# A two-layer graph network on one core: the boundary between the layers reworked (residual joins, a separate normalised tile, order of the dots, scores made ahead of their maxima)

## The chip, the cores and the metric

The kernel runs on one core of one Trainium2 chip. The metric is the device time of that core in microseconds (us), the median of several executions. Before the change it is 3235.16 us, the median of three runs between 3231.14 and 3235.99. All arithmetic on tensors is in fp32; masks are kept in bf16.

## The reference

There are 2708 rows of width 1024 and an adjacency matrix `adj`. Cut to what matters:

```python
h = relu(layernorm(x))                        # layer 0
e = relu((h @ Wf + bf) @ (h @ Wg + bg).T)
a = softmax(where(adj > 0, e, NEG), axis=1)
x = x + a @ (h @ W0 + bW)

h = relu(layernorm(x))                        # layer 1
hW = h @ W1
f1, f2 = hW @ a1, hW @ a2
e = leaky_relu(f1 + f2.T, 0.2)
a = softmax(where(adj > 0, e, NEG), axis=1)
x = x + relu(a @ hW)
```

A leaky relu is monotonic. So the largest score of a row of layer 1 is the leaky relu of `f1` plus the largest `f2` among its neighbours. The kernel needs the maximum of `f2` over the neighbours only, not the scores, to find the shift of the softmax. It must know `f2` of all rows before that maximum is final, and the last rows of `x` come out of the last projection of layer 0.

## The kernel before

**Tiles.** The rows are 22 tiles of up to 128 (`NT`), taken in 11 pairs (`NQ`, `pairs`; one pair consists of the two short tiles of 74 rows). The same rows as targets are five panels, 586, 586, 512, 512 and 512 columns wide (`panels`, `width`). Scores lie transposed: source rows on the partitions, targets of one panel along the free axis. Every large product is made by a Strassen scheme with seven products M1 to M7, in the order M1, M5, M2, M6, M3, M7, M4 in `accumulate` (L466), so the two tiles of a pair are its halves.

**Stages.** In layer 0 each panel p goes through `scores` (L917 matmuls), a softmax, `aggregate(0, p)` (L478, TensorE banks `gx`, `gy`, `gz`, `gv`) and `project(0, p)` (L821, banks `px`, `py`, `pz`). The projection multiplies with `W`, and its `finish0` adds the residual `x_res`, stores the new rows `x1_d` (L1083) and calls `rows_done` (L1023). For the rows of the first four panels, `rows_done` puts the moments, the normalisation, two dots and the Strassen sums of the pair (`pair_h`, L253) into a list of deferred work. The two dots give `f[0]` (f1) and `f[1]` (f2) of the row, from the normalised row and the vectors `wab`, which are `W1 @ a1` and `W1 @ a2`. The list is called `later`: `put` appends to it, `behind(rate)` emits what the credit allows between TensorE products, and `flush` empties it.

**The last projection.** It is `project(0, 4, by_pair=True)`. It takes the two pairs of panel 4 one after the other, so that the rows of the first pair are done while the second is multiplied. `rows_done` then doesn't defer: it emits `normalize`, the dots for `f[0]`, the dots for `f[1]`, `raise_max` for panel 0 (L876, `mx` = the larger of `mx` and mask plus f2) and `pair_h` at once. After the last tile `shifts1` (L1005) turns `mx` on TensorE (`column_max`, L646, bank `mx_ps`), reduces it to one maximum per column (`mcol`), and makes two small columns `z` and `m` from f1 and that maximum. `weights1` (L1128) spreads them over the partitions (`spread`, L205: transposes of a broadcast column into `sp_ps`, then a copy on alternately VectorE and ScalarE) into `ub` and `vb`. Then, one tile at a time, it makes the weights `P`: an Identity pass on ScalarE (L1144), a fused add and maximum and the addition of the mask on VectorE, an exp on ScalarE (L1147). The running sum `sm` follows two tiles later. `aggregate(1, 0)` starts with `gx` on the first tile of `P`.

**What sets the order.** A scheduler decides the order on each engine, from the program's order and the dependences, save where an instruction is held in program order (loads, and VectorE within `scores`). Each engine then works through its queue in that order. VectorE's adds and small operations are recorded under one helper, so all of VectorE's instructions show line L44, and one tells them apart by the tile names. SyncE's queue issues all loads (L121), in order. GpSimd's queue issues the stores and adds `bW` to `x_res` (L1078).

**Buffers.** There are 54 equal `slot` buffers (scores, weights, residuals, temporaries), 12 `stream` buffers (operands loaded from HBM), and 8 PSUM banks. A tile's buffer is free when its last reader is done.

**Lines touched.** `normalize` (L242) works in place: its two Relu passes on ScalarE write into the residual tile that `go` in `finish0` has just sent off to `x1_d`. In `project` (L787) the first product is copied from `px` to `pt` by ScalarE (L827), since M2 accumulates into the same bank after that. M5 and M6 are added to this copy; each of M3, M7 and M4 is added to one of the three sums and then to the residual, two additions each:

```python
o = {M3: M6, M7: M5, M4: M1}[m]
add(t(o), ps, t(o))
finish(tb if m != M3 else ta, 0 if m == M4 else 1, t(o))
```

Of the kernel before, what the change touches and what calls it, by code (L numbers as in the profile page):

```python
# [17 lines left out]
ALPHA = 0.2  # L18
# [38 lines left out]
def kernel(  # L57
# [141 lines left out]
    def halves(t):  # L199
        return [t[:, e * W:(e + 1) * W] for e in range(2)]  # L200
# [23 lines left out]
    def columns_of(p, col):  # L224
        return [col[:n, i:i + 1] for i, (_, n) in enumerate(panels[p])]
# [13 lines left out]
        nc.scalar.activation(rs[:n, :1], mv[:n, 1:2], AF.Sqrt, bias=eps[:n])  # L239
        of_rows[id(t)] = mv, rs  # L240

    def normalize(t):  # L242

        n = t[0].shape[0]
        if id(t) not in of_rows:
            moments(t)
        mv, rs = of_rows.pop(id(t))
        nc.vector.reciprocal(rs[:n, :1], rs[:n, :1])
        nc.vector.tensor_scalar(rs[:n, 1:], mv[:n, :1], rs[:n, :1], -1.0, op0=OP.mult, op1=OP.mult)
        for e in range(2):  # L250
            nc.scalar.activation(t[e], t[e], AF.Relu, bias=rs[:n, 1:], scale=rs[:n, :1])

    def pair_h(l, q, ha, hb):  # L253

# [532 lines left out]
    def project(l, p, G, finish, then={}, by_pair=False, rate=2.0):  # L787

        full = width[p] // P
        col = lambda i, n: [t[:, :, i * P:i * P + n] for t in G]  # L790
        todo = [(first[p] + i, first[p] + i + 1, P, col(i, P), col(i + 1, P)) for i in range(0, full, 2)]
        if p == panel_of[short[0]]:
            n = tiles[short[0]][1]
            for e in range(2):
                nc.scalar.copy(carry[:, e, :, :n], G[e][:, :, full * P:full * P + n])
        if p == panel_of[short[1]]:
            n = tiles[short[1]][1]
            todo.append((*short, n, [carry[:, e, :, :n] for e in range(2)], col(full, n)))
        start_of, finish = finish
        ws = {m: load_W(l, m) for m in (M1, M2)}  # L800
        start_of([t for g in todo for t in g[:2]])
        lefts = []
        for ta, tb, n, (a11, a12), (a21, a22) in todo:
            s = [slot(f"ps{i}", (P, NH, P))[:, :, :n] for i in range(4)]
            add(s[0], a21, a22)
            sub(s[1], s[0], a11)
            sub(s[2], a11, a21)
            sub(s[3], a12, s[1])
            lefts.append({M1: a11, M2: a12, M5: s[0], M6: s[1], M7: s[2], M3: s[3], M4: a22})
        for group, left in (zip([[t] for t in todo], [[t] for t in lefts]) if by_pair else [(todo, lefts)]):  # L810
            acc, tmp = {}, {}
            for m in (M1, M2, M5, M6, M3, M7, M4):
                start = m in (M1, M5, M6)
                w_ = ws.pop(m) if m in ws else load_W(l, m)
                which = "x" if m in (M1, M2) else "y" if m in (M5, M3) else "z"
                for i, (ta, tb, n, _, _) in enumerate(group):
                    if start:
                        acc[which, i] = bank(f"p{which}")
                    ps = acc[which, i][:n]
                    for k in range(NH):  # L820
                        nc.tensor.matmul(ps, left[i][m][:, k, :], w_[k], start=(start and k == 0), stop=(k == NH - 1),  # L821
                                         skip_group_check=True)
                    if start:
                        tmp[m, i] = slot(f"pt{m}")
                    t = lambda m: tmp[m, i][:n, :W]
                    if m == M1:
                        nc.scalar.copy(t(M1), ps)  # L827
                    elif m == M2:
                        finish(ta, 0, ps)
                    elif m in (M5, M6):  # L830
                        add(t(m), ps, t(M1))
                    else:
                        o = {M3: M6, M7: M5, M4: M1}[m]
                        add(t(o), ps, t(o))
                        finish(tb if m != M3 else ta, 0 if m == M4 else 1, t(o))
                    behind(rate)
                if m in then:
                    then.pop(m)()
# [166 lines left out]
    def shifts1(p, between=None):  # L1005

        k, t0 = len(panels[p]), first[p]
        top = column_max(p, mx[p], between)[:, :k]
        f1 = f[0][:, t0:t0 + k]
        z, m, c = (stats.tile([P, 5], FP, name=nm)[:, :k] for nm in ("z", "m1", "none"))  # L1010
        nc.vector.tensor_add(z, f1, top)
        nc.vector.scalar_tensor_tensor(m, z, ALPHA, z, op0=OP.mult, op1=OP.max)
        nc.vector.tensor_scalar(c, top, -BIG / 2, None, op0=OP.is_ge)
        nc.vector.tensor_mul(m, m, c)
        nc.vector.tensor_scalar(c, top, -BIG / 2, -BIG, op0=OP.is_lt, op1=OP.mult)
        nc.vector.tensor_add(m, m, c)
        sub(z, f1, m)
        nc.vector.scalar_tensor_tensor(m, f1, ALPHA, m, op0=OP.mult, op1=OP.subtract)
        return z, m

    done_rows, first_mask = {}, {}

    def rows_done(t, xt):  # L1023

        n = tiles[t][1]
        done_rows[t] = xt

        def dots(k):
            dot(f[k][:n, t:t + 1], xt, [b[:n] for b in halves(wab[k])])
            if k == 1:  # L1030
                nc.vector.tensor_scalar(f2s[:n, t:t + 1], f[1][:n, t:t + 1], ALPHA, None, op0=OP.mult)

        q, k = pair_of[t]
        whole = all(s in done_rows for s in pairs[q])
        if panel_of[t] == NP - 1:
            normalize(xt)
            dots(0)
            dots(1)
            raise_max(0, q, k, first_mask[t][:n, :width[0]])
            if whole and q == NQ - 1:  # L1040
                nc.scalar.activation(stats.tile([P, 1], FP, name="warm"), eps, AF.Exp)
            if whole:
                if q == NQ - 1:
                    got["zm"] = shifts1(0, lambda: pair_h(1, q, *(done_rows[s] for s in pairs[q])))
                else:
                    pair_h(1, q, *(done_rows[s] for s in pairs[q]))
                for p in range(1, NP):
                    put_max(p, q)
            return

        def met():
            known.add(q)
            for p in range(NP):
                if generated[p] > q:
                    put_max(p, q)
        put(1.5, lambda: moments(xt))
        put(0.5, lambda: normalize(xt))
        put(1.6, lambda: dots(0))
        put(1.6, lambda: dots(1))
        if whole:  # L1060
            put(2.7, lambda: pair_h(1, q, *(done_rows[s] for s in pairs[q])))
            put(0.0, met)

    def finish0(p):
# [15 lines left out]
        def go(t, e, c):  # L1080
# [3 lines left out]
            seen[t] = seen.get(t, 0) + 1  # L1084
            if seen[t] == 2:
                rows_done(t, xs[t])
        return start, go

    got = {}
    generated = [0] * NP  # L1090

    def take_max(p):
        got["m"] = column_max(p, got["acc"])
# [6 lines left out]
    for p in range(NP):  # L1100
# [4 lines left out]
        if p + 1 < NP:  # L1105
            B = project_q(p + 1, hooks)
        else:
            project(0, p - 1, G.pop(p - 1), finish0(p - 1), hooks)
        if p == 0:
            prepare_W()  # L1110
        then = {}
# [13 lines left out]
    project(0, NP - 1, G.pop(NP - 1), finish0(NP - 1), by_pair=True, rate=0.0)  # L1125


    def weights1(p, z, m):  # L1128

        w = width[p]  # L1130
        ub, vb1, sm = slot("ub"), slot("vb1"), slot("sm")
        spread(ub, columns_of(p, z))
        spread(vb1, columns_of(p, m))
        S = [None] * NT
        order = [(q, k) for k in range(2) for q in range(NQ)]
        exps[0] = 0

        def go(i, mk):
            if i < len(order):
                q, k = order[i]  # L1140
                n, t = rows_of[q], pairs[q][k]
                S[t] = slot("P")
                s = S[t][:n, :w]
                nc.scalar.activation(s, vb1[:n, :w], AF.Identity, bias=f2s[:n, t:t + 1])  # L1144
                nc.vector.scalar_tensor_tensor(s, ub[:n, :w], f[1][:n, t:t + 1], s, op0=OP.add, op1=OP.max)
                add(s, s, mk[0][:n, :w])
                nc.scalar.activation(s, s, AF.Exp)  # L1147
            if i >= LAG:
                q, k = order[i - LAG]
                total(p, sm, S[pairs[q][k]], rows_of[q], i == LAG)  # L1150
            exps[0] += 1

        front = []
        for i in range(len(order) + LAG):
            mk = []
            front.append([2.1, (lambda i=i, mk=mk: mk.append(load_mask(p, *order[i]))) if i < len(order) else None,
                          (lambda i=i, mk=mk: go(i, mk)), False, None])
        later[:0] = front
        return S, sm

    def finish1(p):
# [9 lines left out]
        def go(t, e, c):  # L1171
# [2 lines left out]
            nc.scalar.activation(o, c, AF.Relu)  # L1174
            add(xs[t][e], xs[t][e], o)
            nc.gpsimd.dma_start(out[r0:r0 + n, e * W:(e + 1) * W], xs[t][e])
        return start, go

    def take_shifts(p):
        flush()  # L1180
# [42 lines left out]
```

## Time and profile before

The profiled execution has a span of 3235.3 us with a mean granted clock of 0.987. Some parts of it, in us from its start:

| stretch | from | to | length |
|---|---|---|---|
| aggregate(0, 4) | 2016.5 | 2151 | 134.3 |
| last projection, pair 1 | 2150.8 | 2175.9 | 25.1 |
| last projection, pair 2 | 2175.9 | 2208.5 | 32.6 |
| last product to the first matmul of layer 1's aggregate | 2208.5 | 2233.85 | 25.3 |
| `gx` of aggregate(1, 0), 88 matmuls | 2233.85 | 2257.6 | 23.8 |

A timeline row gives the start, the length, the engine, line and operation, the tiles written and read with their shapes, and how many instructions were taken together; in brackets stand the engine's idle time before it and who released it. A row of waits gives the engine, line and tile, the releaser, the total wait, how many there were, and the longest. A row of windows gives the stretch and then the busy time of each engine with its count of instructions, the clock granted to TensorE (1.00 is full), the share of time that the DMA engines were busy, and GB/s.

### The profile page before, as it was taken

What the parts mean: (1) busy time and instruction counts of PE and PEld (TensorE: products, weight loads), DVE (VectorE), ACT (ScalarE), POOL (GpSimd) and SP (SyncE); (2) the same over time, 40 slices, a digit from 0 to 9 for tenths busy, and PEclk for the clock granted to TensorE, in tenths of its full rate; (3) what the DMA queues carried; (4) which work ended last, traced back from release to release, by engine and by line L of the source; (5) the groups of instructions that cost most, each with busy time, mean ns of one, the idle gap of its engine ahead of it and who ended that gap; (6) DMA issues with size and microseconds to landing.
All of it is one profiled execution on the core that took longest, in us unless ns stands there. A gap on an engine that the chain in (4) does not pass through costs nothing. (4 is left out here: it accounts for less than half of the span.)

```text
span 3235.3 us, 35363 instructions
## 1 busy us (share of the span) xinstructions
PE 3137.1 (97%) x12924; PEld 2333.4 (72%) x12924; DVE 1756.3 (54%) x3594; ACT 507.7 (16%) x853; POOL 395.0 (12%) x476
## 2 busy tenths in 40 slices
PE   8999999999999999999999998997999999999998
PEld 5577767667876578876888885864767748778585
DVE  7857594275812766327581358537574272553712
ACT  4412120010200102001020002003131030211200
POOL 3723110210002100021000101020010000000001
PEclk9999999999999999999999999998999999999999
DMA  6958866576445575457745565665555445555546
GB/s 262 332 174 297 276 229 227 171 243 215 141 130 163 173 247 190 151 191 242 228 156 156 165 209 185 225 237 200 198 161 175 148 159 171 186 189 175 194 150 212
DMA packets 279628, 641.43 MB, mean 198 GB/s; under 512 B 50686, under 2 KB 116178, under 8 KB 279456
## 3 DMA queue, kind: packets, MB, share of 16 engines
q1 hardware_dynamic: 245184, 525.56, 50.5%
q0 software_dynamic: 34272, 113.62, 9.4%
q8 instruction: 102, 1.67, 0.2%
q14 instruction: 70, 0.57, 0.1%
HBM read 525.49 MB, written 113.58 MB: 198 GB/s over the span
## 5 line engine op out<-in xcount | busy, mean ns | idle before, releaser
L917 PE MATMUL sz<-B,As 128*128 128x256 f32 (+3 forms) x1320 | 328.9, 399 | 5.3 <-DVE st L44 5.3
L917 PEld LDWEIGHTS sz<-B,As 128*128 128x128 f32 (+1 forms) x1320 | 248.7, 189 | 64.5 <-DVE st L44 6.4
L917 PE MATMUL sx<-B,As 128*128 128x256 f32 (+3 forms) x880 | 227.0, 401 | 14.2 <-DMA As<-hs_d 12.0
L756 POOL TENSOR_TENSOR gT<-gT,rr 128x2048 f32<-128x2048 f32 (+3 forms) x20 | 68.3, 3433 | 1320.5 <-DVE rr L44 700.2
L917 PE MATMUL sy<-B,As 128*128 128x256 f32 (+3 forms) x880 | 219.5, 392 | 0.0
L478 PE MATMUL gy<-T,hc 128*128 128x256 f32 (+3 forms) x880 | 205.7, 395 | 6.6 <-DMA hc<-hg_d 6.6
L478 PE MATMUL gx<-P,hc 128*128 128x256 f32 (+3 forms) x880 | 204.5, 394 | 4.7 <-ACT P L1147 4.7
L478 PE MATMUL gz<-Sa,hc 128*128 128x256 f32 (+3 forms) x880 | 206.6, 394 | 0.0
L478 PE MATMUL gz<-P,hc 128*128 128x256 f32 (+3 forms) x880 | 206.3, 393 | 0.0
L917 PEld LDWEIGHTS sx<-B,As 128*128 128x128 f32 (+1 forms) x880 | 162.3, 189 | 51.4 <-issue 11.2
L478 PEld LDWEIGHTS gy<-T,hc 128*128 128x128 f32 (+1 forms) x880 | 168.5, 192 | 42.3 <-DVE junk L44 4.4
L478 PEld LDWEIGHTS gx<-P,hc 128*128 128x128 f32 (+1 forms) x880 | 168.4, 192 | 40.9 <-ACT P L1147 5.0
L917 PEld LDWEIGHTS sy<-B,As 128*128 128x128 f32 (+1 forms) x880 | 163.9, 186 | 38.2 <-issue 0.9
L478 PEld LDWEIGHTS gz<-Sa,hc 128*128 128x128 f32 (+1 forms) x880 | 165.6, 190 | 31.8
L478 PEld LDWEIGHTS gz<-P,hc 128*128 128x128 f32 (+1 forms) x880 | 165.6, 190 | 31.8
L821 PE MATMUL px<-w,gT 128*128 128x512 f32 x320 | 147.3, 613 | 11.5 <-issue 10.0
L821 PE MATMUL py<-w,ps 128*128 128x512 f32 (+1 forms) x352 | 155.6, 593 | 0.3 <-DVE mcol L44 0.3
L821 PE MATMUL pz<-w,ps 128*128 128x512 f32 (+1 forms) x352 | 155.0, 592 | 0.0
L616 ACT COPY mask<-mk_ps 128x1024 bf16<-128x1024 bf16 (+1 forms) x55 | 55.6, 1011 | 575.8 <-PE mk_ps L615 254.6
L821 PEld LDWEIGHTS pz<-w,ps 128*128 128x128 f32 (+1 forms) x352 | 65.5, 186 | 85.6 <-issue 81.7
L821 PEld LDWEIGHTS py<-w,ps 128*128 128x128 f32 (+1 forms) x352 | 65.4, 186 | 85.6 <-issue 82.7
L821 PEld LDWEIGHTS px<-w,gT 128*128 128x128 f32 x320 | 62.5, 197 | 89.2 <-issue 85.3
(240 smaller groups left out, 4797.9 us busy)
## 6 DMA issues: line engine op xcount, KB each, us to landing
hc<-hg_d SPq DMA_DIRECT2D x350, 512.0 KB
As<-hs_d SPq DMA_DIRECT2D x150, 512.0 KB
w<-wt_d SPq DMA_DIRECT2D x96, 512.0 KB
w<-in_L_gnn_W_dram SPq DMA_DIRECT2D x72, 512.0 KB
md<-md_d SPq DMA_DIRECT2D x56, 512.0 KB
adj_i<-in_adj_dram SPq DMA_DIRECT2D x50, 512.0 KB
hg_d<-g POOLq DMA_DIRECT2D x40, 512.0 KB, 5.0
hs_d<-hsT POOLq DMA_DIRECT2D x40, 512.0 KB, 5.6
```

Source lines behind the costliest of these rows:

```text
L478: nc.tensor.matmul(ps[d], left(m, k, d), right(m, k), start=(start and k == 0), stop=(k == K - 1), skip_group_check=True)
L616: nc.scalar.copy(mk[:n, :, :k4 * P], ps[:n, :, :k4 * P])
L756: nc.gpsimd.tensor_tensor(of(e, s), of(e, s), by(s, k), OP.mult)
L821: nc.tensor.matmul(ps, left[i][m][:, k, :], w_[k], start=(start and k == 0), stop=(k == NH - 1), skip_group_check=True)
L917: nc.tensor.matmul(ps[:n, :h], lefts[q][:, i % 2, c, :n], B[m][c // 2][:, c % 2, :h], start=(start and c == 0), stop=(c == NH - 1), skip_g ...
```

## The change

It has five parts, all around the boundary between the layers.

- **Residual joined early.** In the pair-wise layer-0 projection, and in the other layer-0 projections too, the three sums of the first products are added to the residual tiles as soon as the M6 product is there (`join`). The later products M3, M7 and M4 are then added from PSUM to the residual directly. The work between the last product and the finished row is one addition, where it was two.
- **First copy.** In the pair-wise layer-0 projection VectorE, not ScalarE, copies the first product out of `px`.
- **Last rows' relu into its own tile.** In panel 4 `normalize` writes into new tiles `h_last`, so that it doesn't overwrite a residual tile whose store is on its way.
- **The maximum's dot first.** `rows_done` makes the dots for `f[1]` and the update of `mx` before the dots for `f[0]`. The short exp that brings in ScalarE's table (`warm`) is held in program order behind the last normalisation. In `shifts1` two comparisons no longer share a tile and stand ahead of the chain.
- **Scores ahead of their maxima.** Behind project(0, 3), `scores_before` makes the scores of panel 0 of layer 1 without a shift, for the first tiles of those pairs that lie wholly in panels 0 to 3. It does so in the deferred list during aggregate(0, 4), from `f1` spread over the partitions (`f1b`), with leaky relu as the larger of s and 0.2 s, and the mask. These tiles stay in their buffers. After the maxima are known `weights1` spreads the shift (`mb`), subtracts it from such a tile and takes the exp. The columns `z` and `c` for the other tiles are spread later, when the first such tile is met.

```diff
-    def normalize(t):
+    def normalize(t, into=None):
...
-            nc.scalar.activation(t[e], t[e], AF.Relu, bias=rs[:n, 1:], scale=rs[:n, :1])
+            nc.scalar.activation((into or t)[e], t[e], AF.Relu, bias=rs[:n, 1:], scale=rs[:n, :1])
...
+        copy1 = nc.vector.tensor_copy if by_pair and l == 0 else nc.scalar.copy
...
+                    o = {M3: M6, M7: M5, M4: M1}.get(m)
                     if m == M1:
-                        nc.scalar.copy(t(M1), ps)
+                        copy1(t(M1), ps)
                     elif m == M2:
                         finish(ta, 0, ps)
-                    elif m in (M5, M6):
+                    elif o is None:
                         add(t(m), ps, t(M1))
-                    else:
-                        o = {M3: M6, M7: M5, M4: M1}[m]
+                    elif join is None:
                         add(t(o), ps, t(o))
                         finish(tb if m != M3 else ta, 0 if m == M4 else 1, t(o))
+                    else:
+                        finish(tb if m != M3 else ta, 0 if m == M4 else 1, ps)
+                    if join and m == M6:
+                        join(tb, 1, t(M5))
+                        join(ta, 1, t(M6))
+                        join(tb, 0, t(M1))
...
         nc.vector.tensor_add(z, f1, top)
+        nc.vector.tensor_scalar(c, top, -BIG / 2, None, op0=OP.is_ge)
+        nc.vector.tensor_scalar(d, top, -BIG / 2, -BIG, op0=OP.is_lt, op1=OP.mult)
         nc.vector.scalar_tensor_tensor(m, z, ALPHA, z, op0=OP.mult, op1=OP.max)
-        nc.vector.tensor_scalar(c, top, -BIG / 2, None, op0=OP.is_ge)
         nc.vector.tensor_mul(m, m, c)
-        nc.vector.tensor_scalar(c, top, -BIG / 2, -BIG, op0=OP.is_lt, op1=OP.mult)
-        nc.vector.tensor_add(m, m, c)
+        nc.vector.tensor_add(m, m, d)
...
-            normalize(xt)
-            dots(0)
+            done_rows[t] = row_halves("h_last", n)
+            normalize(xt, done_rows[t])
+            if whole and q == NQ - 1:
+                tc.keep_in_program_order(nc.scalar.activation(stats.tile([P, 1], FP, name="warm"), eps, AF.Exp))
             dots(1)
             raise_max(0, q, k, first_mask[t][:n, :width[0]])
-            if whole and q == NQ - 1:
-                nc.scalar.activation(stats.tile([P, 1], FP, name="warm"), eps, AF.Exp)
+            dots(0)
...
+    def scores_before():
+
+        w = width[0]
+        f1b = slot("f1b")
+
+        def go(q, mk):
+            n, t = rows_of[q], pairs[q][0]
+            before[t] = slot("P")
+            s = before[t][:n, :w]
+            nc.scalar.activation(s, f1b[:n, :w], AF.Identity, bias=f2s[:n, t:t + 1], scale=ALPHA)
+            nc.vector.scalar_tensor_tensor(s, f1b[:n, :w], f[1][:n, t:t + 1], s, op0=OP.add, op1=OP.max)
+            add(s, s, mk[0][:n, :w])
+        spread(f1b, columns_of(0, f[0]))
+        for q in range(NQ):
+            if panel_of[pairs[q][0]] < NP - 1 and panel_of[pairs[q][1]] < NP - 1:
+                mk = []
+                put(1.8, lambda q=q, mk=mk: go(q, mk), lambda q=q, mk=mk: mk.append(load_mask(0, q, 0)))
...
+        if p == 0:
+            mb = slot("mb")
+            spread(mb, columns_of(p, shift))
+        else:
+            spreads()
...
+                if p == 0 and t in before:
+                    S[t] = before.pop(t)
+                    s = S[t][:n, :w]
+                    sub(s, s, mb[:n, :w])
+                else:
+                    if p == 0 and not spreaded:
+                        spreads()
+                        spreaded.append(True)
...
                 nc.scalar.activation(s, s, AF.Exp)
```

More of the change, by code (lines that the diff above doesn't have):

```diff
@@ L798, in project @@
             todo.append((*short, n, [carry[:, e, :, :n] for e in range(2)], col(full, n)))
-        start_of, finish = finish
+        start_of, join, finish = finish
         ws = {m: load_W(l, m) for m in (M1, M2)}
@@ L1009, in shifts1 @@
         f1 = f[0][:, t0:t0 + k]
-        z, m, c = (stats.tile([P, 5], FP, name=nm)[:, :k] for nm in ("z", "m1", "none"))
+        z, m, c, d = (stats.tile([P, 5], FP, name=nm)[:, :k] for nm in ("z", "m1", "none", "m2"))
         nc.vector.tensor_add(z, f1, top)
+        nc.vector.tensor_scalar(c, top, -BIG / 2, None, op0=OP.is_ge)
+        nc.vector.tensor_scalar(d, top, -BIG / 2, -BIG, op0=OP.is_lt, op1=OP.mult)
         nc.vector.scalar_tensor_tensor(m, z, ALPHA, z, op0=OP.mult, op1=OP.max)
-        nc.vector.tensor_scalar(c, top, -BIG / 2, None, op0=OP.is_ge)
         nc.vector.tensor_mul(m, m, c)
-        nc.vector.tensor_scalar(c, top, -BIG / 2, -BIG, op0=OP.is_lt, op1=OP.mult)
-        nc.vector.tensor_add(m, m, c)
+        nc.vector.tensor_add(m, m, d)
         sub(z, f1, m)
-        nc.vector.scalar_tensor_tensor(m, f1, ALPHA, m, op0=OP.mult, op1=OP.subtract)
-        return z, m
+        nc.vector.scalar_tensor_tensor(c, f1, ALPHA, m, op0=OP.mult, op1=OP.subtract)
+        return z, c, m
     done_rows, first_mask = {}, {}
@@ L1028, in dots @@
         def dots(k):
-            dot(f[k][:n, t:t + 1], xt, [b[:n] for b in halves(wab[k])])
+            dot(f[k][:n, t:t + 1], done_rows[t], [b[:n] for b in halves(wab[k])])
             if k == 1:
@@ L1086, in go, with join @@
                 rows_done(t, xs[t])
-        return start, go
+        def join(t, e, c):
+            add(xs[t][e], xs[t][e], c)
+        return start, join, go
     got = {}
     generated = [0] * NP
+    before, spreaded = {}, []
+    def scores_before():
[13 more added lines that the diff above has]
+                put(1.8, lambda q=q, mk=mk: go(q, mk), lambda q=q, mk=mk: mk.append(load_mask(0, q, 0)))
     def take_max(p):
@@ L1108 @@
             project(0, p - 1, G.pop(p - 1), finish0(p - 1), hooks)
+            scores_before()
         if p == 0:
@@ L1125, with weights1, spreads @@
     project(0, NP - 1, G.pop(NP - 1), finish0(NP - 1), by_pair=True, rate=0.0)
-    def weights1(p, z, m):
+    def weights1(p, z, m, shift):
         w = width[p]
         ub, vb1, sm = slot("ub"), slot("vb1"), slot("sm")
-        spread(ub, columns_of(p, z))
-        spread(vb1, columns_of(p, m))
+        def spreads():
+            spread(ub, columns_of(p, z))
+            spread(vb1, columns_of(p, m))
+        if p == 0:
[3 more added lines that the diff above has]
+            spreads()
         S = [None] * NT
@@ L1141, in go @@
                 n, t = rows_of[q], pairs[q][k]
[L1142 to L1146, printed above, removed]
+                if p == 0 and t in before:
[6 more added lines that the diff above has]
+                        spreaded.append(True)
+                    S[t] = slot("P")
+                    s = S[t][:n, :w]
+                    nc.scalar.activation(s, vb1[:n, :w], AF.Identity, bias=f2s[:n, t:t + 1])
+                    nc.vector.scalar_tensor_tensor(s, ub[:n, :w], f[1][:n, t:t + 1], s, op0=OP.add, op1=OP.max)
+                    add(s, s, mk[0][:n, :w])
                 nc.scalar.activation(s, s, AF.Exp)
@@ L1155, in weights1 @@
             mk = []
-            front.append([2.1, (lambda i=i, mk=mk: mk.append(load_mask(p, *order[i]))) if i < len(order) else None,
+            front.append([2.1, (lambda i=i, mk=mk: mk.append(load_mask(p, *order[i])))
+                          if i < len(order) and not (p == 0 and pairs[order[i][0]][order[i][1]] in before) else None,
                           (lambda i=i, mk=mk: go(i, mk)), False, None])
@@ L1176, in go @@
             nc.gpsimd.dma_start(out[r0:r0 + n, e * W:(e + 1) * W], xs[t][e])
-        return start, go
+        return start, None, go
     def take_shifts(p):
```

## The prediction

> **What bounds the kernel now.** I read the page's first part, the PE waits, then the PE and ScalarE timelines from the last layer-0 product to the first layer-1 aggregate, and stage windows.
>
> The first part says that TensorE (PE) sets the span: 97% busy. So only PE's idle time, its slow clock and its instruction count can move the result.
>
> ```profile
> PE 3137.1 (97%) x12924; PEld 2333.4 (72%) x12924; DVE 1756.3 (54%) x3594; ACT 507.7 (16%) x853; POOL 395.0 (12%) x476
> ```
>
> PE's waits (total us, times, longest): at the boundary lie `mx_ps`, `sp_ps`<-z, `gx`<-P, the 4.8 of `px` and two of the four of `pz`.
>
> ```profile
> PE mx_ps L654 <- DVE mx L44: 14.8, 1, 14.8
> PE px L821 <- issue: 10.0, 3, 4.8
> PE pz L821 <- DVE pt L44: 5.1, 4, 2.7
> PE gx L478 <- ACT P L1147: 4.7, 1, 4.7
> PE sp_ps L213 <- DVE z L44: 2.2, 1, 2.2
> ```
>
> PE's timeline (start, length, operation, idle before it) shows two holes: 4.83 us inside pair 2 of the last projection, and 14.80+2.16+4.72 between its last product (ends 2208.5) and `gx` at 2233.85.
>
> ```profile
> 2185.16 6.11 PE L821 MATMUL px<-w,gT 128*128 128x512 f32 x8 [4.83 <-issue]
> ...
> 2204.92 3.70 PE L821 MATMUL pz<-w,gT 128*128 128x512 f32 x8 [0.78 <-DVE pt L44]
> 2223.42 1.33 PE L654 MATMUL mx_ps<-ident,mx 128*128 128x128 f32 x5 [14.80 <-DVE mx L44]
> 2226.91 1.24 PE L213 MATMUL sp_ps<-ident,z 128*128 128x128 f32 x5 [2.16 <-DVE z L44]
> 2227.94 1.18 PE L213 MATMUL sp_ps<-ident,m 128*128 128x128 f32 x5
> 2233.85 23.94 PE L478 MATMUL gx<-P,hc 128*128 128x293 f32 x88 [4.72 <-ACT P L1147]
> ```
>
> ScalarE (ACT) explains the holes: the copy of `px` queued behind pair 1's normalisations; a normalisation that waits for the store of its tile; then spreads, three score passes and a table load ahead of the first exp.
>
> ```profile
> 2184.50 0.56 ACT L827 COPY pt<-px 128x512 f32<-128x512 f32 x1
> ...
> 2217.47 0.81 ACT L251 ACTIVATE x_res<-x_res,rs 128x512 f32<-128x512 f32 x1 [3.06 <-DMA x_d<-x_res]
> ...
> 2229.66 2.13 ACT L1144 ACTIVATE P<-vb,f2s 128x586 f32<-128x586 f32 x3
> 2231.81 1.28 ACT L1147 ACT_TABLE_LOAD   x1
> ```
>
> Windows (PE busy, DVE, ACT, POOL after it, then granted clock, DMA share, GB/s): `gx` begins at half clock; PE alone at the program's start follows for step 6.
>
> ```profile
> 2233.80:2236.00 2.20, 2.15 (x5) 1.55 (x6) 2.06 (x4) 1.60 (x3) 0.00 (x0) 0.50 0.25 67
> 2236.00:2238.00 2.00, 2.00 (x6) 1.42 (x5) 1.90 (x4) 2.00 (x4) 0.00 (x0) 0.54 0.90 271
> 2238.00:2240.00 2.00, 2.00 (x10) 1.55 (x9) 2.00 (x4) 1.78 (x4) 0.00 (x0) 1.00 1.01 395
> ```
>
> ```profile
> 16.00:18.00 2.00, 2.00 (x9) 0.50 1.03 422
> 18.00:20.00 2.00, 2.00 (x4) 0.70 1.02 386
> 20.00:22.00 2.00, 2.00 (x6) 1.00 1.06 401
> ```
>
> **The Trainium skill.** "TensorE: Matmul & The Clock Gate", Part 1: the array falls to half rate after an idle window and returns after some 3.4 us of sustained work. The trace agrees: after both holes 0.50 for about 4 us. That page's passage on transposes says they don't count as busy in the same way; the start speaks against it: work resumes at 15.26 with 2.4 us of transposes, and the clock is back by 19.2. "ScalarE: Activation LUTs", What ACT_TABLE_LOAD costs: about 1283 ns; the trace has 1.28. "PSUM — Partial Sum Buffer", Engine vs sequencer instructions: ScalarE, VectorE and GpSimd queues are strict FIFO, which is how the `px` copy above came to hold PE.
>
> **The change, part by part**, in order of time; DVE row prices: 512-wide add, dot half or bn_stats about 0.65 net of overlap, 586-wide maximum 0.75, tiny operations 0.1 to 0.2.
>
> 1. *Scores made early*, beside aggregate(0,4). Nine tiles, each with an ACT pass 0.70 and DVE 0.82+0.75: 14.1 us of DVE. PE is full throughout that aggregate (19.00 of 19 us in each window), while DVE is 19.0, 10.3, 12.6, 1.7, 7.5, 2.4, 2.9 busy: 76 of 134 us free. The running maxima slide later, into the empty windows. Cost 0. On PE five transposes of `f1` are added; four such took 0.43 us before `gv` (2131.36 to 2131.79): +0.5.
>
> 2. *Joins.* In the pair-wise projection three of the second adds move off the last product, DVE's count stays at nine. In project(0,3), where DVE was saturated and `pz` waited 2.74, summing DVE's queue from the softmax's start to the add that frees `pz` gives 32.7 us against 33.2 before: 0, ±0.6.
>
> 3. *Last pair-wise products.* The add that frees `pz` for M4 now stands behind the first dot half of the same rows, since these dots start earlier: the wait of 0.78 becomes about 1.4, on both pairs: +0.6 each.
>
> 4. *px copy on DVE.* It now follows all of pair 1's tail. M4 of pair 1 would end at 2176.5, the residual add at 2177.4, bn 2178.1, moments, sqrt and reciprocal 2179.2, two normalisations of 0.81 2180.8; then on DVE four dot halves, one maximum and four 0.65 adds of `pair_h`, the copy last, at 2186.9. On ACT it ended at 2185.1. PE's second `px` product thus starts at 2186.9, not 2185.16: +1.8, the 0.6 of pair 1 included. The hole is about 6 us, its cold stretch stays.
>
> 5. *From the last product to gx.* It ends at 2208.5+1.8+0.6=2210.9. One add instead of two (-0.7) gives 2211.7; bn, moments, sqrt, reciprocal 2213.5; two normalisations into their own tile, without the 3.06 wait, 2215.1; second dot half for `f[1]` 2215.8, add of g 2216.5, a half of the other dot, maximum 2218.1 (the other dot no longer lies wholly ahead of it); `mx_ps` 2219.4. DVE is then still at a dot half and three g adds until 2220.8, which costs 1.4; `mcol` (1.08) 2221.9; shifts, shorter by 0.2 with the two comparisons ahead, 2222.8. Transposes of `mb` and its copy end 1.73 later by before's pace (2226.91 to the end of `ub`, 2228.64): 2224.5; one subtract 0.7, exp 0.70: 2226.1. The other ten transposes end by then too (3.2 us in all). The 2.13 of score passes, the second copy and the 1.28 load, now behind the last normalisation, are off the path. gx starts at 2226.1 against 2233.85: **-7.7**, with steps 3 and 4 inside.
>
> 6. *Clock.* `gx` took 23.94 for 88 matmuls; the same groups later take 21.7, so 2.2 went to the cold start. Now 15 transposes run for 3.2 us right up to `gx`. By the program's start they count, and about 0.6 would be left: -1.6. By the skill's passage 0. I take -1.6; both ends stay.
>
> 7. *First tiles of P.* DVE needs a subtract and a sum per tile, about 1.4 us, PE 8 matmuls, 1.97 us: no starvation. At the start one dot is queued ahead of copies that PE awaits: 0 to 0.6, I take 0.2.
>
> Sum: -7.7 -1.6 +0.5 +0.2 = -8.6, so 3235.2-8.6 = **3226.6 us**.
>
> **Rivals.**
> - *A, the clock doesn't come back.* Step 6 is 0, and the start and project(0,3) cost 0.6 each: -7.7+0.5+1.2=-6.0, 3229.2. For it: the skill's passage; small transposes are thin work. Against: the start. 25%.
> - *B, DVE keeps better time.* If g adds and copy fit into waits for ACT, step 4 is 0 and `mcol` isn't held: -8.6-1.8-1.4=-11.8, 3223.4. For it: DVE has gaps of 0.9 for ACT there. Against: FIFO order, the copy is last. 15%.
> - *C, a new wait in aggregate(0,4).* Nine mask loads (146.5 KB) and nine held buffers come earlier, and the maxima's loads are paced by DVE on the queue that also issues `hc`. If each of M7's six `hc` loads came 2 us late, +12: 3238.6, slower. For it: `gy` waited 6.6 us for `hc` in two places in this kernel. Against: PE never waited in this aggregate, and DMA there is at 0.47 to 0.95. 10%.
> - The forecast: 50%.
>
> **Numbers.** Faster by 0.2% means under 3228.7. Forecast and B lie there (65%), and a fair part of A by its spread: 0.70; same, most of A, 0.21; slower, C with no more than a wait partly eaten, 0.09. The range reaches from B's far side (steps 6 and 4 both better) 3221.5 to between A and C, 3234.5.
>
> **What would show it.** `gx`'s wait on DVE or ACT after `sp_ps` near 1 us or below; last pz to `gx` near 15.2 us against 25.3; `gx` x88 near 22.3; no `x_d` store among ACT's waits; the second `px` hole at 6 us with DVE as releaser; `gx`, `gy`, `gz`, `gv` of aggregate(0,4) still without waits. Wrong: an `hc` or mask wait there, or the hole in pair 2 beyond 7 us.

## The result and the profile after

The changed kernel takes 3223.27 us, the median of six runs (3218.51 to 3225.68), against 3233.29 for six runs of the kernel before. The measured ratio is 0.9966, with a 95% interval of 0.9954 to 0.9979 (the two medians give 0.9969): some 10 us, or 0.3%, faster. The forecast was 3226.6 us, in a range from 3221.5 to 3234.5.

The first line of the changed kernel's page has ten more TensorE instructions and 5.6 us less TensorE busy time. Of these 5.6 us, 3.8 lie ahead of the last projection, where scatter between executions is as large (see below).

```profile
PE 3131.5 (97%) x12934; PEld 2330.3 (72%) x12934; DVE 1765.3 (55%) x3607; ACT 507.1 (16%) x853; POOL 396.2 (12%) x476
```

TensorE's waits, as before (total, times, longest):

```profile
PE px L822 <- issue: 11.1, 3, 5.9
PE mx_ps L654 <- DVE mx L44: 7.1, 1, 7.1
PE pz L822 <- DVE x_res L44: 5.9, 3, 3.3
```

`mx_ps` fell from 14.8 to 7.1 us, and the 4.7 of `gx` for P is gone. The `px` wait rose from 10.0 to 11.1, and `pz` has three waits for `x_res`, of which 3.3 lies in project(0, 3) and the other two at the boundary. TensorE's timeline from the hole (its idle time) in pair 2 to layer 1:

```profile
2178.84 6.22 PE L822 MATMUL px<-w,gT 128*128 128x512 f32 x8 [5.90 <-issue]
...
2199.27 3.70 PE L822 MATMUL pz<-w,gT 128*128 128x512 f32 x8 [1.34 <-DVE x_res L44]
2210.10 1.33 PE L654 MATMUL mx_ps<-ident,mx 128*128 128x128 f32 x5 [7.12 <-DVE mx L44]
2214.39 1.24 PE L213 MATMUL sp_ps<-ident,m 128*128 128x128 f32 x5 [2.96 <-DVE m L44]
2215.42 1.18 PE L213 MATMUL sp_ps<-ident,z 128*128 128x128 f32 x5
2216.40 1.19 PE L213 MATMUL sp_ps<-ident,none 128*128 128x128 f32 x5
2217.71 22.16 PE L478 MATMUL gx<-P,hc 128*128 128x293 f32 x88
```

The page gives no releaser for the hole, but VectorE's timeline does: its copy of `px` ends just before the product starts.

```profile
2178.05 0.68 DVE L44 COPY pt<-px 128x512 f32<-128x512 f32 x1
```

Fifteen transposes now lead into `gx`, with no wait between them and it. ScalarE shows why: at the boundary no normalisation waits for a store, the table load follows the last normalisation, and one copy, VectorE's subtraction and one pass (the exp) lie between the transposes and P.

```profile
2205.60 1.52 ACT L251 ACTIVATE h_last<-x_res,rs 128x512 f32<-128x512 f32 x2 [0.54 <-DVE rs L44]
2207.14 1.28 ACT L1046 ACT_TABLE_LOAD   x1
...
2215.54 0.58 ACT L156 COPY mb<-sp_ps 128x512 f32<-128x512 f32 x1 [6.90 <-PE sp_ps L213]
2216.96 2.05 ACT L1193 ACTIVATE P<-P 128x586 f32<-128x586 f32 x3 [0.84 <-DVE P L44]
```

**Where the trace must be read with care.** The two profiled executions differ by 18.6 us in span (3235.3 and 3216.7), though the medians differ by 10.0. The last projection already starts 8.1 us earlier after the change (2142.73 against 2150.79), behind stages that the change hardly touches. The third experiment below runs the same program as the kernel before up to that point, and there it starts at 2144.84. So scatter between executions alone makes 5.95 us here. The five other kernels below that share the changed kernel's program up to that point start it between 2145.62 and 2148.19, so no part of the 8.1 us can be told from scatter.

Where the 5.95 us lie can be read from the two traces. TensorE idled 55.4 us up to that point in the kernel before and 55.5 in the third experiment, but was busy for 2095.4 and 2089.3 us with the same matmuls. Of this work 41.5 us ran at half clock in the one and 29.1 in the other; half of that difference is 6.2 us. The windows of one place, `scores` of panel 2 after a wait for `As`, show a part of it (stretch, TensorE's busy time, granted clock, DMA share, GB/s): the kernel before, and then the third experiment.

```profile
1160.00:1165.00 5.00, 5.00 (x12) 0.50 1.03 407
```

```profile
1160.00:1165.00 5.00, 5.00 (x24) 1.00 1.04 406
```

Where the clock fell, 12 matmuls were done and not 24. The wait was 2.84 us in the first and 2.06 in the second, but its length alone doesn't decide: in the same place a wait of 2.10 us (the own tile alone, below) was followed by half clock, and one of 2.59 (the changed kernel) wasn't.

Hence the stretches below are all counted from the start of the last projection, and two stretches are kept apart: to the start of `gx`, and from there to `gy`, which depends on when the clock comes back. The first holds a cold stretch too where there is a hole: the second `px` product behind it took between 5.07 and 6.67 us, so that stretch can differ by over 1 us for this reason alone.

| kernel | hole in pair 2 | projection's start to `gx` | `gx` to `gy` | time, us |
|---|---|---|---|---|
| before | 4.83 | 83.06 | 23.77 | 3233.3 |
| changed | 5.90 | 74.98 | 21.99 | 3223.3, ratio 0.9966 |
| copy on ScalarE | 0.30 | 66.53 | 23.11 | 3217.0, ratio 0.9944 (0.9930 to 0.9957) |
| the same, late additions | 0.31 | 64.88 | 22.23 | 3211.8, ratio 0.9935 (0.9922 to 0.9947) |
| before, with fill | 4.72 | 82.94 | 22.04 | 3230.8, one run |
| changed, no scores ahead | 5.96 | 77.42 | 24.80 | 3229.7, one run |
| changed, relu in place | 8.34 | 85.43 | 21.87 | 3234.5, one run |
| changed, f1's dot first | 5.91 | 76.26 | 23.01 | 3224.4, one run |
| changed, no join | 7.35 | 76.15 | 22.85 | 3226.4, one run |
| late additions, f1's dot first | 0.31 | 65.93 | 23.07 | 3215.0, one run |
| before, own tile alone | 1.86 | 73.89 | 24.29 | 3225.7, ratio 0.9971 (0.9962 to 0.9980) |
| late additions, join in last panel | 0.32 | 64.90 | 23.17 | 3213.9, ratio 0.9939 (0.9925 to 0.9952) |

All ratios are to the kernel before. One of eleven runs of the own tile alone took 5224.2 us at a mean granted clock of 0.59, where the others had 0.988 or more, and is left out. A single run can't tell 5 us, so there the two stretches are the measurement. They come from one trace of each kernel.

### The profile page after: what moved, and what is told of

Same layout as the page of the kernel before. It is cut to its first block, busy times and chain, and to the rows that moved or that the text cites. A ratio compares the mean times of both kernels' runs of the same rounds, so it can differ in the third digit from the quotient of the medians.

```text
span 3216.7 us, 35402 instructions
## 1 busy us (share of the span) xinstructions
PE 3131.5 (97%) x12934; PEld 2330.3 (72%) x12934; DVE 1765.3 (55%) x3607; ACT 507.1 (16%) x853; POOL 396.2 (12%) x476
## 5 line engine op out<-in xcount | busy, mean ns | idle before, releaser
L822 PE MATMUL px<-w,gT 128*128 128x512 f32 x320 | 145.8, 608 | 12.6 <-issue 11.1
```

## The experiments

### The copy of px on ScalarE again

```diff
-        copy1 = nc.vector.tensor_copy if by_pair and l == 0 else nc.scalar.copy
+        copy1 = nc.scalar.copy
```

> The changed kernel with one part undone: the first product of the pair-wise layer-0 projection is copied by ScalarE again, not VectorE. Theory (the 5.90 us hole in pair 2 is VectorE's queue alone): with the normalisations no longer waiting for stores, ScalarE is free 0.2 us before px is complete or just after (2172.73 against 2172.94 in the changed kernel's trace), so the hole falls from 5.9 to about 0.4 us, TensorE doesn't fall to half clock, and the second px product takes 3.6 instead of 6.2 us: 8.0 us less, about 3215 us. The stretch from the first product of the last projection to gy of layer 1 falls from 97.0 to 89.0 us. Rival (pair 1's tail bounds pair 2 in any case, as VectorE must add px and py too): the hole moves to the next product, at least 3 us of wait and a cold clock remain, less than 3 us gained.

ScalarE's timeline of this kernel around the copy:

```profile
2176.12 1.52 ACT L251 ACTIVATE h_last<-x_res,rs 128x512 f32<-128x512 f32 x2 [0.48 <-DVE rs L44]
2177.55 0.56 ACT L829 COPY pt<-px 128x512 f32<-128x512 f32 x1
```

and TensorE's second `px` product, at 2178.21, waited 0.30 us and took 3.67 us at full clock. The stretch to `gx` is 8.45 us shorter than in the changed kernel, and the time is 6.2 us lower. The theory holds, and with it a judgement on the change: moving this copy to VectorE cost 8.45 us of what the other parts brought. In the kernel before the copy was late because ScalarE's queue had been held by the store, as the run with the own tile alone shows below. This is ScalarE's row in the kernel before, in pair 1:

```profile
2175.62 0.81 ACT L251 ACTIVATE x_res<-x_res,rs 128x512 f32<-128x512 f32 x1 [3.32 <-DMA x_d<-x_res]
```

Once the store no longer holds the relu, ScalarE is the engine that is free, and VectorE's tail (four dot halves, a maximum, four additions) is the longer queue.

### The Strassen sums of the last pair behind the maxima

On top of the former kernel `pair_h` of the last pair is emitted behind the first three tiles of P, and VectorE's order is held there.

```diff
-                    got["zm"] = shifts1(0, lambda: pair_h(1, q, *(done_rows[s] for s in pairs[q])))
+                    nc.hold = True
+                    got["zm"] = shifts1(0)
+                    got["late"] = lambda: pair_h(1, q, *(done_rows[s] for s in pairs[q]))
...
         def go(i, mk):
+            if i == 3 and "late" in got:
+                got.pop("late")()
+                nc.hold = False
```

> As the run with the copy on ScalarE, and in addition the four VectorE additions for the Strassen sums of the last pair are made behind the first weights of layer 1, not ahead of the column maxima. Theory (VectorE is the bound from the last normalisation to mcol): one addition goes from ahead of the last maximum (0.6 us) and three from ahead of mcol (1.2 us until mx_ps is there): from the last product to gx 14.8 becomes 13.0 us, 1.8 us less than the run before it, about 3213 us. Rival (the additions were hidden behind the transposes, or they come back as waits of gx for P): no gain, or gx's 88 matmuls take longer than 22.2 us.

```profile
2208.59 1.24 PE L213 MATMUL sp_ps<-ident,m 128*128 128x128 f32 x5 [1.78 <-DVE m L44]
...
2211.91 22.39 PE L478 MATMUL gx<-P,hc 128*128 128x293 f32 x88
```

TensorE waits 1.78 us for the shift here, 2.96 in the former kernel. From the last product to `gx` it takes 13.11 us (14.77 in the former kernel), and 64.88 us from the projection's start, 1.65 less. (The end of the last product is taken here and below as 3.60 us after its start; by the rows' own lengths it lies 0.1 us later in every kernel.) `gx`'s 88 matmuls waited for nothing. The theory holds, and this is the fastest kernel of the study: 3211.83 us, 11.4 below the changed kernel. The edit also holds VectorE's order there; what that does alone was not tested.

### Transposes as work for the clock

```diff
         spread(vb1, columns_of(p, m))
+        if p == 0:
+            ps = bank("fill")
+            for i in range(20):
+                j = slice(i % 4 * P, i % 4 * P + P)
+                nc.tensor.transpose(ps[:, j], vb1[:, j], ident)
```

> The kernel before, with 20 transposes of 128x128 added that nothing reads, on TensorE between the spread of m and gx, where it waited 4.72 us for P. Theory (TensorE's activity brings the clock back, transposes too): gx starts when it did, and its 88 matmuls and the start of gy come 21.9 to 22.2 us later instead of 23.8, 1.7 us less. Rival (transposes don't count as work for the clock): 23.8 us as before, with 0.50 in the first 4 us.

TensorE's timeline and windows (stretch, PE busy, granted clock, DMA share, GB/s) of this kernel:

```profile
2223.61 4.01 PE L1138 MATMUL fill<-ident,vb 128*128 128x128 f32 x20 [0.55 <-ACT vb L156]
2227.78 22.20 PE L478 MATMUL gx<-P,hc 128*128 128x293 f32 x88 [0.16 <-ACT P L1152]
```

```profile
2224.60:2226.60 2.00, 2.00 (x11) 0.50 0.06 23
2226.60:2227.80 1.20, 1.04 (x9) 0.86 0.15 22
2227.80:2229.80 2.00, 2.00 (x8) 1.00 0.20 62
```

`gx` starts where it did (82.94 us after the projection's start, 83.06 before), but at full clock, and `gy` follows 22.04 us later, not 23.77. Nothing but transposes ran in the 6 us ahead of the full clock. They do count as work here, in disagreement with the Trainium skill ("TensorE: Matmul & The Clock Gate", Part 4), by which a transpose doesn't count as busy in the same way.

### No scores ahead of their maxima

```diff
-            scores_before()
...
-        if p == 0:
-            mb = slot("mb")
-            spread(mb, columns_of(p, shift))
-        else:
-            spreads()
+        spreads()
+        spreaded.append(True)
```

> The changed kernel without the scores made ahead of their maxima; layer 1's first weights are made from z and c as in the kernel before. Theory: from the first transposes of the spread to gx 3.3 us become 6.5 (one more copy, Identity pass 0.7, fused add and maximum 0.8, mask 0.75), +3.2; TensorE then idles 4 us ahead of gx, so the clock is cold again and gx to gy takes 23.7 instead of 22.0, +1.7; the five transposes of f1 are gone, -0.5. The stretch from the first product of the last projection to gy grows from 97.0 to 101.9. Rival (the early scores cost as much in aggregate(0, 4) as they bring): aggregate(0, 4) is over 3 us shorter than the 134.4 us of the changed kernel.

The stretch to `gx` grew by 2.44 us, not 3.2, and `gx` to `gy` by 2.81, not 1.7:

```profile
2219.69 1.24 PE L213 MATMUL sp_ps<-ident,z 128*128 128x128 f32 x5 [3.17 <-DVE z L44]
...
2226.28 24.96 PE L478 MATMUL gx<-P,hc 128*128 128x293 f32 x88 [4.38 <-ACT P L1189]
```

From the spread to `gx` lie 6.59 us, as expected (3.32 with the early scores); the stretch grew by less because the clock came back sooner behind the hole, and the second `px` product took 5.07 us, not 6.22. Behind the 4.38 us of idle time the clock came back 6.1 us after `gx` began. That took 4.0 us in the kernel before and 5.0 with the own tile alone, after waits of 4.72 in both, so some 1 us of the 2.81 is scatter. aggregate(0, 4), from its first matmul to the first of the projection, takes 134.31 us here, 134.36 with the early scores and 134.31 before: they are hidden, and the rival is out.

### The relu in place again

```diff
-            done_rows[t] = row_halves("h_last", n)
-            normalize(xt, done_rows[t])
+            normalize(xt)
```

> The changed kernel with one part undone: the last rows' relu writes into the residual tile again. Theory (the store holds the relu): after each pair's last product one normalisation waits some 3 us for the store of the half that it overwrites, as 3.32 and 3.06 in the kernel before. VectorE's tail of pair 1 and with it the copy of px come 3 us later, so the hole in pair 2 grows from 5.9 to about 9 us, and from the last product to gx 14.8 becomes 17.9; first product of the last projection to gy 103 us against 97.0. Rival (VectorE is the bound there and has other work to do in the wait, as the additions for the sums): under 1 us in each place, 98 to 99 us.

The hole is 8.34 us, near the 9 of the theory, but from the last product to `gx` it takes 22.44 us, not 17.9. The stretch to `gx` is 85.43, 10.45 more than with the separate tile and 2.4 more than in the kernel before. Theory and rival were both too low. ScalarE's timeline in pair 2 shows waits for two stores in a row, not one:

```profile
2210.09 0.81 ACT L251 ACTIVATE x_res<-x_res,rs 128x512 f32<-128x512 f32 x1 [3.90 <-DMA x_d<-x_res]
...
2222.77 0.81 ACT L251 ACTIVATE x_res<-x_res,rs 128x512 f32<-128x512 f32 x1 [3.55 <-DMA x_d<-x_res]
```

The first wait is for the store of the pair's first tile. VectorE has the second half of that tile's dot next in its queue, so the residual addition of the last product, ready at 2211.2, is made at 2214.43. Only then can the second tile be stored, normalised and wait again.

### The order of the dots

```diff
-            dots(1)
-            raise_max(0, q, k, first_mask[t][:n, :width[0]])
             dots(0)
+            dots(1)
+            raise_max(0, q, k, first_mask[t][:n, :width[0]])
```

> The changed kernel with one part undone: the dots for f1 ahead of those for f2 and the maximum. Theory: VectorE has the same work up to mcol, four dot halves, one maximum and four additions, but now none of it is left to run beside the transposes of mx (1.2 us from their start to mcol): from the last product to gx 14.8 becomes 16.0, and the hole in pair 2 stays at 5.9. Rival A (VectorE's total decides, order is worth nothing): 14.8. Rival B (the two dot halves count in full): 16.2 and more with their small operations.

From the last product to `gx`: 16.14 us, hole 5.91. The theory holds: the order brings 1.3 us, since half a dot and three additions run on VectorE while TensorE turns the maxima.

> The kernel with the copy on ScalarE and the late additions, with the dots for f1 ahead of those for f2 and the maximum. Theory: without the additions only one half of the dot for f1 stood ahead of the maximum's dots and one behind; now both halves and a small operation are ahead: the maximum is 0.75 us later, and mcol, which waited for mx_ps, too: 13.1 becomes 13.9 from the last product to gx. Rival (the order is worth two dot halves): 14.4 or more.

The same edit on the kernel with late additions gives 14.15 us from the last product to `gx` against 13.11, which is 1.04 more (0.75 expected, 1.3 for the rival), in between. By this the order is worth about 1 us with the additions or without.

### No early join

```diff
-        return start, join, go
+        return start, None, go
```

> The changed kernel with one part undone: M3, M7 and M4 are added to the sums and then to the residual, two additions each. Theory: one addition more stands behind each last product, +0.7 from the last product to gx (14.8 to 15.5) and in pair 1's tail (hole 5.9 to 6.5), but the add that frees pz for M4 stands ahead of the dot again, so M4 waits 0.78 instead of 1.3 twice. First product of the last projection to gy 97.0 becomes 97.4. Rival (the addition counts in full in both pairs): 98.4.

M4 waits 0.78 us instead of 1.3, as expected, but the hole is 1.45 us longer and the last product to `gx` 1.50. Less the 0.5 by which M4 came earlier, that is 0.95 in each pair; 0.74 came back by chance, as the second `px` product took 5.48 us and not 6.22, and 1.17 are left in the stretch to `gx`. So the rival was nearer: in both pairs the addition (0.69 us on VectorE) counts in full, and a little more. M4's longer wait had cost at most 0.3 us, because in the changed kernel VectorE waited only 0.30 us for the last product.

The page of waits named a third wait for `x_res`, in project(0, 3). So the join was tried in the last panel alone, on the kernel with late additions:

```diff
-        return start, join, go
+        return start, join if p == NP - 1 else None, go
```

> The kernel with the copy on ScalarE and the late additions, and the early join of the residual in the last panel only. Theory: in project(0, 3), where VectorE has work without pause, the joins put more ahead of the add that frees pz, whose wait was 2.74 before, 3.32 with the joins and 2.30+0.17 in the changed kernel without them: about 2.5, 0.8 us less in all, and the boundary stays as it was (64.9 us from the first product of the last projection to gx). The time can hardly tell: about 3211 us. Rival (the order of VectorE's queue there moves with everything else): the wait stays at 3.3.

In project(0, 3) `pz` waits 2.29+0.17 us, where it waited 3.31, and the stretch to `gx` is 64.90. The theory holds for the stage. The time, 3213.86 us, can't be told from 3211.83.

### The own tile alone

The kernel before, with `into` in `normalize` and `h_last` in `rows_done`, and nothing else.

> The kernel before with one part of the change alone: the last rows' relu writes into its own tile. Theory (the store's hold on the relu, through VectorE's and ScalarE's queues, is most of what the boundary lost): pair 1's last add no longer waits behind a dot for it, so ScalarE's copy of px comes 3.0 us earlier, the hole in pair 2 falls from 4.83 to about 1.9 us, the clock doesn't fall there (another 2.5 us), and the last maximum comes 2.4 us earlier (3.06 less what VectorE did in the wait). From the first product of the last projection to gx 83.06 becomes 75.2, about as with all five parts (74.98); about 3225 us. Rival (the parts add up, and this one is worth its 3.06): 80.0, about 3230 us.

```profile
2181.49 3.67 PE L821 MATMUL px<-w,gT 128*128 128x512 f32 x8 [1.86 <-issue]
...
2213.55 1.33 PE L654 MATMUL mx_ps<-ident,mx 128*128 128x128 f32 x5 [11.04 <-DVE mx L44]
```

The hole is 1.86 us and the second `px` product runs at full clock. The stretch to `gx` is 73.89 us, shorter than with all five parts (74.98). Of the 9.17 us that this part alone brings, 2.97 lie in the hole, 2.44 in the product behind it and 3.76 in the wait ahead of `mx_ps` (11.04, not 14.80). The theory holds, and the parts don't add up: this one alone brings 9.2 us up to `gx`, all five 8.1, and all without the copy on VectorE 16.5. The copy on VectorE in the kernel before, with nothing else, was not tried.

## Why the prediction was right

Along its steps:

- **Step 1, early scores.** Right: aggregate(0, 4) is 134.36 us long against 134.31, without a wait. The five transposes of f1 took 0.50 us (2007.87 to 2008.37). Rival C is out.
- **Step 2, joins.** The wait for VectorE in project(0, 3) went from 2.74 to 3.32 us, the upper edge of the ±0.6; the sum of VectorE's queue had said 0. It is 3.35 without the early scores and 2.30+0.17 without the joins, so the joins do it.
- **Step 3, M4's waits.** Measured 1.28 and 1.34 us, against 1.4. The size was right and the charge of 0.6 for each was not: without the joins these waits were 0.78, and the last addition came no earlier. VectorE waited 0.3 us for the product, so no more than that can count.
- **Step 4, the px copy.** Hole 5.90, forecast about 6, and the cold clock stayed; the releaser on the page is not VectorE, as forecast, but VectorE's copy ends where the hole ends. The step took the place of the copy as given. Two runs show what it hid: the hole came from the store in the kernel before, and without the copy on VectorE it would have closed.
- **Step 5, last product to gx.** 14.84 us, forecast 15.2. That VectorE's dot half and three additions hold `mcol` was seen, and priced at 1.4. With late additions, and with the dots reversed, TensorE's wait for the shift fell from 2.96 to 1.78 and 1.77 us, so the hold was there and cost 1.2. Together, steps 3 to 5 gave -8.1 up to `gx` where -7.7 was forecast.
- **Step 6, the clock.** `gx` to `gy` fell by 1.78 us, forecast 1.6, and the fill shows the cause, so rival A is out. The size isn't firm: in the eight kernels that have the same transposes ahead of `gx` it lies between 21.87 and 23.17, and in the three that wait over 4 us there it is 23.77, 24.29 and 24.80. The groups don't overlap and their means differ by 1.6 us, but that one pair of traces came so near the forecast is luck.
- **Its sums.** Three slips, none over 1 us. The 2.2 us of cold start in step 6 set a row's length (23.94) against a distance between starts (21.7); lengths alone give 23.94-21.88 = 2.06. In step 5, 2224.5 plus 0.7 and 0.70 is 2225.9, not 2226.1; from the copy of `mb` to `gx` the trace has 1.59 us, so 2226.1 fits it better. And the half clock lasted 4.9 us behind the hole in pair 2, not about 4; behind the second it was 4.0.

From the profiled stages this gives -8.1-1.8+0.5+0.6 = -8.8 us, where the forecast was -8.6. The medians give -10.0, with an interval of the ratio that reaches from -6.8 to -14.9. The start of the program, forecast at +0.2, can't be told from scatter: TensorE's wait for `wgT` was 4.1 before and 3.5 after.

Why the same wait drops the clock in one execution and not in another was not tested; what the traces show of it stands at the end.

## What to carry to other kernels

In this kernel a store holds the tile that it reads: the relu in place behind it waited until the transfer was done (up to 3.9 us at the boundary). The wait is handed on to every engine that has something queued behind it, so it can be worth more than the idle time shown beside it: 9.2 us here, where the two longest waits were 3.32 and 3.06. Parts of a change that remove the same wait don't add up; ask of each what it would bring once the others are in, since here moving a copy off a queue that was no longer held cost 8 us. Where an engine is last to arrive, a wait of another engine beside it costs little (M4's waits above), and taking work off the late engine (four additions that nobody needed yet) is what pays.

## What the runs showed of the hardware

- The half clock came back at different times after the first transposes ahead of `gx`: 3.7 us in the changed kernel and 6.0 with the copy on ScalarE, with the same instructions in the same rhythm, and between 3.5 and 6.1 us in the eight kernels that have them. The Trainium skill ("TensorE: Matmul & The Clock Gate", Part 1) says that the window runs free and that the cold stretch varies from run to run; these traces agree. They also show steps: in all twelve the stretches at half clock, save the one at the program's end, are whole multiples of 3.41 us long (2207.87 to 2218.11 in the changed kernel is three), and within a trace all of them start on one grid of 3.41 us. This is worth over 1 us of a stage, so differences of that size in `gx` to `gy` are no effect of an edit.
- An idle time of 1.86 us on TensorE left the clock at full, one of 4.83 didn't. In between, its length alone doesn't decide. The wait ahead of the M4 products of project(0, 3) was 2.74 us in the kernel before, with the fill and with the own tile alone. Only in the first did the clock fall: these products took 8.83 us there and 7.13 in the others. With a wait of 3.31 to 3.35 us it fell in five of seven traces.
